# Attention in units of four steps instead of pairs, with the other products gathered in one slot of two

## Chip, core and metric

The kernel runs on one core of a Trainium2 chip. The metric is the device time of one execution in microseconds (us). Before the change it is 806.05 us, the median of 3 runs (804.99 to 806.32).

## The reference

The input x is 2 batches of 2048 tokens of 256 values, float32. All arithmetic is in float32.

```python
x = x + layernorm(attention(layernorm(x)))      # layernorm inside, 4 heads of 64, q and k RMS-normed
x = x + layernorm(ffn(layernorm(x)))
# attention: softmax(qn kn^T) v for each head and batch, then w_o and b_o
# ffn: scores = x gate_w^T; chosen = argmax over 8 experts; x + x expert_w[chosen]^T
```

The feed-forward part sends each token through one expert of eight, so tokens have to be sorted by expert before full tiles of them can be multiplied.

## The kernel before, in words

There are two paths, chosen by a test on the gains of q and k; the one that runs is `bounded_path`, and only this one is meant below. The scores are bounded there, so that the softmax needs no maximum: `exp(s - bound)` is summed as it comes.

**Attention.** One step is a batch, a block of 512 queries, a pair of heads and a tile of 128 keys: 2 x 4 x 2 x 16 = 256 steps. `scores` (L1034) issues a step's two matmuls on TensorE, one for each head, each over 64 rows (tile s, two buffers of two banks), and the exponential on ScalarE that makes the tile p (five buffers). `add` (L1075) adds p into acc on VectorE; acc's column sums become the softmax's denominators. `weigh` (L1087) issues the step's two matmuls with the values, each into 64 of the rows of po (one bank, summed over 16 steps). A float32 matmul appears in the trace as two records, so a step has four records of s and four of po. After 16 steps po is copied to oT (L1129), and `block_sums` (L1051) takes acc's sums with a ones matrix (tile sm, L1056), and in four parts the reciprocals and the products with oT on VectorE.

**Other work.** The remaining work is cut into Python generators that stand in a queue with a slot number at which they begin: `project` (norm, products for q, k and v and their transposes, for one tile of tokens: 32 in all), `expert_weights`, `tokens` (after two blocks of heads: the output projection py on TensorE, the norm, the choice of the expert on VectorE, in two parts one slot apart; in the last rows of a group one tile of tokens per slot, otherwise one in four), `order` (the routing of a group: the matmuls rank, a chain of small VectorE instructions, a slot later a second chain, and later the matmuls src), `places` (one tile of tokens of one expert: gather, transposes pt_g, product pe, norm) and `collect` (gather of the finished rows, residual, output). Group A is the first batch, group B the first three blocks of the second. `between` (L926) is one slot: it moves each running generator one step on. A step ends at a `yield`; a `yield then(...)` runs on in the same slot, a `yield later(...)` or a bare `yield` ends the slot for that generator. The `Next` that a yield gives names the engine of the next step, its cost and what it takes. Before the change only the planner of the end (`finish`, L944) uses it.

**The order.** The engines' order is the order in which the code issues (a manual schedule), and each engine works through its own queue in that order. The loop at L1111 runs over pairs of steps. In each round it issues the scores of the next pair, the adds of the present pair, one slot of other work, and the values of the present pair:

```python
ahead = [scores(i) for i in following]
for i, p in zip(mine, held):
    add(i, p)
between(now)
now += 1
for i, p in zip(mine, held):
    weigh(i, p)
held = ahead
```

Other matmuls share three banks (`ps_m`, L344). After the last pair, `finish` plans what is left by estimated costs.

Of the kernel before, what the change touches and what calls it, by code (L numbers as in the profile page):

```python
# [25 lines left out]
def kernel(  # L26
# [23 lines left out]
    NT = N // P  # L50
# [223 lines left out]
    def bounded_path():  # L274
# [76 lines left out]
        class Next(NamedTuple):  # L351
# [8 lines left out]
            give: str = ""  # L360
            later: bool = False
            order: int = -1

        then = Next

        def later(*args, **kw):
            return Next(*args, later=True, **kw)
# [58 lines left out]
        def project(bt, t):  # L426


            n = f"{bt.b}_{t}"
            src = x_tile(bt.b * NT + t)  # L430

            mv, _ = moments(src, f"a{n}")
            rs = roots[:, bt.b * NT + t : bt.b * NT + t + 1]
            rsqrt(rs, mv[:, 1:2], 1.0 + LN_EPS, LN_EPS * LN_EPS, ALU.add)
            yield
            xn = wk.tile([P, D], F32, tag="xn", name=f"xn_{n}")
            nc.vector.tensor_scalar(xn, src, mv[:, 0:1], rs, ALU.subtract, ALU.mult)
            yield
            pt = ps_m(f"pt_x{n}")
            for c in range(NCH):  # L440
                nc.tensor.transpose(  # L441
                    pt[:, c * P : (c + 1) * P], xn[:, c * P : (c + 1) * P], ident
                )
            xnT = wk.tile([P, NCH, P], F32, tag="xnT", name=f"xnT_{n}")
            nc.scalar.activation(  # L445
                xnT,
                pt[:, :D].rearrange("p (c n) -> p c n", n=P),
                AF.Identity,
                bias=raised,
            )  # L450
            yield
            pqk = ps_m(f"pqk{n}")
            for c in range(NCH):
                nc.tensor.matmul(  # L454
                    pqk,
                    xnT[:, c, :],
                    wqkT[:, c, :, :].rearrange("p a d -> p (a d)"),
                    start=(c == 0),
                    stop=(c == NCH - 1),
                )  # L460
            pv = ps_m(f"pv{n}")
            for c in range(NCH):
                nc.tensor.matmul(  # L463
                    pv[:, :DG],
                    xnT[:, c, :],
                    wvT[:, c, :],
                    start=(c == 0),
                    stop=(c == NCH - 1),
                )
            qk = wk.tile([P, 2 * D], F32, tag="qk", name=f"qk_{n}", bufs=4)  # L470
            nc.scalar.copy(qk, pqk)  # L471
            nc.scalar.copy(bt.V[:, t, :], pv[:, :DG])
            sq = wk.tile([P, 2 * D], F32, tag="sq", name=f"sq_{n}", bufs=1)
            nc.scalar.activation(sq, qk, AF.Square)
            yield
            ss = small.tile([P, 2 * H], F32, tag="ss", name=f"ss_{n}")
            nc.vector.tensor_reduce(
                ss, sq.rearrange("p (g d) -> p g d", d=DH), AX.X, ALU.add
            )
            rn = small.tile([P, 2 * H], F32, tag="rn", name=f"rn_{n}")  # L480

            rsqrt(rn, ss, 1.0 / DH, RMS_EPS * RMS_EPS, ALU.max)
            yield
            qk3 = qk.rearrange("p (g d) -> p g d", d=DH)
            nc.vector.tensor_tensor(
                qk3, qk3, rn.unsqueeze(2).to_broadcast([P, 2 * H, DH]), ALU.mult
            )
            yield
            pt = ps_m(f"pt_qk{n}")
            for c in range(2 * NCH):  # L490
                nc.tensor.transpose(  # L491
                    pt[:, c * P : (c + 1) * P], qk[:, c * P : (c + 1) * P], ident
                )
            cols = bass.ts(t, P)
            qb, j = divmod(t, QT4)
            if bt.QT[qb] is None:
                bt.QT[qb] = kv.tile([P, NCH, KB], F32, tag="QT", name=f"QT{n}", bufs=NKB + 1)
            pt3 = pt.rearrange("p (c n) -> p c n", n=P)
            qt = bt.QT[qb][:, :, bass.ts(j, P)]
            nc.scalar.activation(  # L500
                bt.KT[:, :, cols], pt3[:, NCH : 2 * NCH, :], AF.Copy, scale=g_k
            )
            if bt.b == 0:
                nc.vector.tensor_scalar(qt, pt3[:, :NCH, :], g_q8, None, ALU.mult)
            else:
                nc.scalar.activation(qt, pt3[:, :NCH, :], AF.Copy, scale=g_q8)
            bt.done.add(t)
            yield

        def expert_weights(e):  # L510
            w = load_raw(raw, expert_w[e], f"we_raw{e}")
            yield
            yield
            wt = raw.tile([P, NCH, D], F32, tag="wraw", name=f"weT{e}")
            turn_weight(w, four(ps_m(f"pt_we{e}")), wt)

            for c in range(NCH):
                own = wt[:, c, c * P : (c + 1) * P]
                nc.vector.tensor_tensor(own, own, ident, ALU.add)
            nc.sync.dma_start(out=weTd[e], in_=wt)  # L520
            yield
# [51 lines left out]
        def order(gr):  # L573
# [3 lines left out]
            ps = ps_m(f"rank{n}")  # L577
# [31 lines left out]
            end = tiles  # L609
            k = 1  # L610
            while k < E:
# [3 lines left out]
                end = more  # L615
# [54 lines left out]
            ps = ps_m(f"src{n}")  # L670
# [15 lines left out]
            for t in range(T):  # L686
                at += 0.5 if at >= len(steps) // PAIR + lead else 1
                g = opens(early(collect(gr, t)), Next("POOL", 1.3), 3, lambda: None if gr.left else gr.written)
                queue.append((at + 4, g))
            queue.sort(key=lambda q: q[0])  # L690
            yield

        def places(gr, j):
# [18 lines left out]
            nc.sync.dma_start(  # L712
                out=w, in_=weTd[bass.ds(e, 1)].rearrange("e p c d -> p (e c) d")
            )
            yield later("PE", 0.3, 3.0, take="mx")
            if attending:
                yield later("PE", 0.3, take="mx", give="mx")
            pt = ps_m(f"pt_g{n}")
            for c in range(NCH):
                nc.tensor.transpose(  # L720
# [202 lines left out]
                if step is None or step is running or step.later:  # L923
                    return step is not running

        def between(now):  # L926
            new = []
            while queue and queue[0][0] <= now:
                new.append(queue.pop(0)[1])
                if new[-1] in firsts:  # L930
                    advance(new[-1])
            old = running[:]
            running.extend(new)
            due = old + [g for g in new if g not in firsts]
            begun.update((g, now) for g in new)


            if 3 < now < NT + 4 or now == 2:
                due.sort(key=lambda g: max(2 - now + begun[g], -1) % 4)
            for g in due:  # L940
                if not advance(g):
                    running.remove(g)

        def finish():  # L944

# [84 lines left out]
        def ready(i):  # L1030
            b, qb, c, kc = steps[i]
            return batches[b].done.issuperset({kc, *range(qb * QT4, (qb + 1) * QT4)})
# [74 lines left out]
        while not all(ready(i) for i in range(PAIR)):  # L1107
            between(now)
            now += 1
        held = [scores(i) for i in range(PAIR)]  # L1110
        for g in range(len(steps) // PAIR):  # L1111
            mine = range(g * PAIR, (g + 1) * PAIR)
            following = [i + PAIR for i in mine if i + PAIR < len(steps)]
            while not all(ready(i) for i in following):
                between(now)
                now += 1
            lead = now - g
            ahead = [scores(i) for i in following]
            for i, p in zip(mine, held):
                add(i, p)  # L1120
            between(now)
            now += 1
            for i, p in zip(mine, held):
                weigh(i, p)
            held = ahead
            b, qb, c, kc = steps[mine[-1]]
            if kc == NT - 1:
                oT = wk.tile([P, KB], F32, tag="oT", name=f"oT{g}", bufs=4)
                nc.scalar.copy(oT, po)  # L1129
                w = opens(block_sums(g, acc, oT), Next("PE", 1.0, take="m"), 0)  # L1130
                queue.append((now, w))
                oTs.append(oT)
                if c == NCH - 1:
                    tt = b * NT + qb * QT4
                    gr = next((g for g in groups if g.first <= tt < g.first + g.T), None)
                    last = gr and tt + QT4 == gr.first + gr.T
                    gap = 1 if last else 4 if following else 1
                    for j in range(QT4):
                        w = tokens(batches[b], qb, j, oTs, gr)
                        end = (len(steps) // PAIR - 1, j)  # L1140
                        opens(w, Next("PE", 0.5, take="m"), 0, lambda end=end: normed.get(end))
                        queue.append((now + 1 + gap * j, w))
                    oTs = []
                queue.sort(key=lambda q: q[0])
# [380 lines left out]
```

## Time and profile before

| what | us |
|---|---|
| median of 3 runs | 806.05 |
| the profiled execution's own time | 805.99 |
| its span, first to last instruction | 804.2 |
| PE busy / DVE busy / ACT busy / POOL busy | 760.8 / 639.4 / 448.8 / 326.2 |
| one exponential p (ACT, 256 of them) | 1.110 |
| one add into acc (DVE, 224 of them) | 1.222 |
| one reciprocal of 128x128 (DVE, 64 of them) | 0.95 |
| TensorE clock granted, mean | 0.978 |

PE is TensorE's matmuls, PEld its weight loads, DVE is VectorE, ACT ScalarE, POOL GpSimd, SP the engine that issues most of the transfers. A row of a timeline gives the start and the length of a group of like instructions in us, the engine, the line, what is written from what, how often, and in brackets how long the engine sat idle before and what ended that. A matmul's length is that of one instruction from its start to its end; since matmuls are pipelined, the step from one start to the next is what it costs.

### The profile page before, as it was taken

What the parts mean: (1) busy time and instruction counts of PE and PEld (TensorE: products, weight loads), DVE (VectorE), ACT (ScalarE), POOL (GpSimd) and SP (SyncE); (2) the same over time, 40 slices, a digit from 0 to 9 for tenths busy, and PEclk for the clock granted to TensorE, in tenths of its full rate; (3) what the DMA queues carried; (4) which work ended last, traced back from release to release, by engine and by line L of the source; (5) the groups of instructions that cost most, each with busy time, mean ns of one, the idle gap of its engine ahead of it and who ended that gap; (6) DMA issues with size and microseconds to landing.
All of it is one profiled execution on the core that took longest, in us unless ns stands there. A gap on an engine that the chain in (4) does not pass through costs nothing.

```text
span 804.2 us, 10268 instructions
## 1 busy us (share of the span) xinstructions
PE 760.8 (95%) x3166; PEld 320.4 (40%) x3166; DVE 639.4 (80%) x1379; ACT 448.8 (56%) x699; POOL 326.2 (41%) x336
## 2 busy tenths in 40 slices
PE   7999999999999999999997999999999996997794
PEld 5545433343334333433332434444443332334551
DVE  2757688789797879688989976878698899975767
ACT  2656655555656555655554455666666543355851
POOL 3634331134253344244324135757545445127114
PEclk8999999999999999999999999999999999899997
DMA  4100211210010000000131413433212343317436
GB/s 128 54 1 26 66 54 52 79 33 20 13 54 15 13 20 20 21 20 20 48 110 60 119 33 105 125 112 112 73 48 77 112 118 98 109 53 255 88 105 193
DMA packets 48686, 57.58 MB, mean 72 GB/s; under 512 B 6408, under 2 KB 39952, under 8 KB 48624
## 3 DMA queue, kind: packets, MB, share of 16 engines
q1 hardware_dynamic: 42064, 44.65, 17.4%
q0 software_dynamic: 3568, 9.32, 4.7%
q10 hardware_dynamic: 2992, 2.88, 1.2%
q8 instruction: 27, 0.44, 0.2%
q14 instruction: 35, 0.29, 0.1%
HBM read 37.69 MB, written 19.14 MB: 71 GB/s over the span
## 4 chain that ended last, share of the span: by engine, by line
PE 75%; DVE 12%; ACT 3%; DMA 3%; issue 3%; POOL 2%; SPq 0%; DVEq 0%; POOLq 0%; ACTq 0%
PE s L1040 24%; PE po L1094 24%; PE pqk L454 7%; PE pv L463 4%; DVE acc L1085 3%; PE peA L730 3%; PE py L793 3%; PE pt_qk L491 2%; PE sm L1056 2%; PE peB L730 1%; PE pt_x L441 1%; DVE acc L1064 1%; PE pe L862 1%; DMA fgA<-fnA,posA 1%; ACT p L1048 1%
## 5 line engine op out<-in xcount | busy, mean ns | idle before, releaser
L1048 ACT ACTIVATE p<-s,nbound 128x1024 f32<-128x1024 f32 x256 | 271.0, 1110 | 182.7 <-PE s L1040 182.7
L1085 DVE TENSOR_TENSOR acc<-acc,p 128x1024 f32<-128x1024 f32 x224 | 273.6, 1222 | 11.5 <-ACT p L1048 1.2
L1040 PE MATMUL s<-QT,KT 64*128 64x512 f32 x1024 | 255.1, 616 | 2.3 <-ACT p L1048 2.3
L1094 PE MATMUL po<-p,V 128*64 128x512 f32 x1024 | 251.5, 612 | 0.2 <-ACT oT L1129 0.2
L1040 PEld LDWEIGHTS s<-QT,KT 64*128 64x128 f32 x1024 | 88.3, 187 | 165.2 <-issue 92.2
L1094 PEld LDWEIGHTS po<-p,V 128*64 128x64 f32 x1024 | 64.1, 138 | 129.2 <-issue 126.9
L374 POOL TENSOR_TENSOR rn<-rs_t,mhalf 128x8 f32<-128x8 f32 x32 | 58.8, 1839 | 74.1 <-DVE rs_t L373 74.1
L374 POOL TENSOR_TENSOR roots<-rs_t,mhalf 128x1 f32<-128x1 f32 x32 | 23.9, 748 | 96.4 <-DVE rs_t L373 96.3
L454 PE MATMUL pqk<-wqkT,xnT 128*128 128x512 f32 x128 | 62.0, 608 | 0.3 <-ACT xnT L445 0.3
L374 POOL TENSOR_TENSOR rs_z<-rs_t,mhalf 128x1 f32<-128x1 f32 x28 | 34.8, 1243 | 59.0 <-DVE rs_t L373 59.0
L374 POOL TENSOR_TENSOR rs_y<-rs_t,mhalf 128x1 f32<-128x1 f32 x28 | 32.2, 1149 | 55.7 <-DVE rs_t L373 49.1
L1064 DVE RECIPROCAL acc<-acc 128x128 f32<-128x128 f32 x45 | 42.5, 944 | 0.0
L837 ACT ACTIVATE x2n<-x,shift_y,rs_y 128x256 f32<-128x256 f32 x28 | 16.8, 599 | 44.0 <-POOL shift_y L391 39.2
L698 POOL DMA_INDIRECT rows<-x2nA,srcA x23 | 29.9, 1298 | 24.3 <-DMA ring<-weTd 18.3
L793 PE MATMUL py<-woT,oT 128*128 128x264 f32 x128 | 35.6, 402 | 0.5 <-ACT xTB L725 0.5
L768 POOL DMA_INDIRECT fgA<-fnA,posA x16 | 19.9, 1243 | 37.9 <-DVE rs_t L373 12.0
L463 PE MATMUL pv<-wvT,xnT 128*128 128x264 f32 x128 | 33.7, 386 | 0.0
L1064 DVE RECIPROCAL acc<-sm 128x128 f32<-128x128 f32 x19 | 18.0, 950 | 18.7 <-PE sm L1056 18.7
L374 POOL TENSOR_TENSOR rs_fA<-rs_t,mhalf 128x1 f32<-128x1 f32 x23 | 18.1, 785 | 36.0 <-DVE rs_t L373 35.0
L471 ACT COPY qk<-pqk 128x512 f32<-128x512 f32 x32 | 18.8, 587 | 22.8 <-PE pqk L454 22.8
L463 PEld LDWEIGHTS pv<-wvT,xnT 128*128 128x128 f32 x128 | 24.3, 190 | 17.6 <-issue 10.8
L698 POOL DMA_INDIRECT rows<-x2nB,srcB x19 | 20.9, 1098 | 22.4 <-DVE srcB L679 16.8
(262 smaller groups left out, 927.9 us busy)
## 6 DMA issues: line engine op xcount, KB each, us to landing
ring<-weTd SPq DMA_DIRECT2D x34, 256.0 KB, 3.0
x<-in_L_attn_x_dram SPq DMA_DIRECT2D x8, 512.0 KB, 4.0
xr<-in_L_attn_x_dram SPq DMA_DIRECT2D x28, 128.0 KB, 2.2
fnA<-fA SPq DMA_DIRECT2D x23, 128.0 KB, 2.4
we_raw<-in_L_ffn_expert_w_dram ACTq DMA_DIRECT2D x8, 256.0 KB, 2.6
weTd<-weT SPq DMA_DIRECT2D x8, 256.0 KB, 2.1
x2A<-x SPq DMA_DIRECT2D x16, 128.0 KB, 1.7
fgA<-x2A SPq DMA_DIRECT2D x16, 128.0 KB, 2.1
```

Source lines behind the costliest of these rows:

```text
L374: nc.gpsimd.tensor_tensor(dst, t[:, :n], mhalf[:, :n], ALU.pow)
L454: nc.tensor.matmul(pqk, xnT[:, c, :], wqkT[:, c, :, :].rearrange("p a d -> p (a d)"), start=(c == 0), stop=(c == NCH - 1),)
L463: nc.tensor.matmul(pv[:, :DG], xnT[:, c, :], wvT[:, c, :], start=(c == 0), stop=(c == NCH - 1),)
L698: nc.gpsimd.indirect_dma_start(out=xg, out_offset=None, in_=gr.x2n[:, :], in_offset=bass.IndirectOffsetOnAxis(ap=gr.src[:, j : j + 1], axi ...
L730: nc.tensor.matmul(pe, xT[:, c, :], w[:, c, :], start=(c == 0), stop=(c == NCH - 1))
L768: nc.gpsimd.indirect_dma_start(out=o, out_offset=None, in_=gr.fn[:, :], in_offset=bass.IndirectOffsetOnAxis(ap=gr.pos[:, t : t + 1], axis= ...
L793: nc.tensor.matmul(py, oT[:, bass.ts(j, P)], woT[:, c, :], start=(c == 0), stop=(c == NCH - 1),)
L1040: nc.tensor.matmul(s[:, r, :], bt.KT[rows, c, bass.ts(kc, P)], bt.QT[qb][rows, c, :], start=True, stop=True,)
L1048: nc.scalar.activation(p, s, AF.Exp, bias=nbound)
L1064: nc.vector.reciprocal(acc[:, 0, cols], share[:, cols])
L1085: nc.vector.tensor_tensor(acc, acc, p, ALU.add)
L1094: nc.tensor.matmul(po[r * DH : (r + 1) * DH, :], batches[b].V[:, kc, h * DH : (h + 1) * DH], p[:, r, :], start=(kc == 0), stop=(kc == NT - 1),
```

## The change

The loop now runs over units of four steps: the scores of two steps, then the adds that the unit before left over, one slot of other work ("few"), the scores of two more steps, the adds of the first two, the values of all four, and one more slot ("rest"). The adds of the last two steps are issued in the next unit after its first scores, or, at the end of a block of 16 steps, directly after the slot "rest". In a slot "few" the steps whose engine is PE go ahead up to three banks or until 2.0 us of estimated work are there; what doesn't fit is put off, and only that goes in the slot "rest". Steps of other engines go in both. As long as the first batch is projected (slots below 20) every slot takes all, and there are two more slots in a unit, among the values.

For this, some steps say that they begin on PE and what they take; `places` waits one slot without a bank in place of holding one, and `collect` begins four slots later.

```diff
+            banks: int = 1
...
             xn = wk.tile([P, D], F32, tag="xn", name=f"xn_{n}")
             nc.vector.tensor_scalar(xn, src, mv[:, 0:1], rs, ALU.subtract, ALU.mult)
-            yield
+            yield later("PE", 0.3)
...
-            yield
+            yield later("PE", 2.7, banks=2)
             pqk = ps_m(f"pqk{n}")
...
-            yield
+            yield later("PE", 0.5)
             pt = ps_m(f"pt_qk{n}")
...
             yield
-            yield
+            yield later("PE", 0.6)
             wt = raw.tile([P, NCH, D], F32, tag="wraw", name=f"weT{e}")
...
-                queue.append((at + 4, g))
+                queue.append((at + 8, g))
...
-            yield later("PE", 0.3, 3.0, take="mx")
             if attending:
-                yield later("PE", 0.3, take="mx", give="mx")
+                yield later("", 0.0, 3.0)
+                yield later("PE", 0.3, take="mx")
+            else:
+                yield later("PE", 0.3, 3.0, take="mx")
             pt = ps_m(f"pt_g{n}")
...
-        def between(now):
+        def between(now, kind="all"):
+            nonlocal put_off
...
+            banks, work, waiting = 0, 0.0, set()
             for g in due:
+                step = nexts.get(g) or opening.get(g)
+                if kind != "all" and step and step.engine == "PE":
+                    full = banks + step.banks > 3 and work < 2.0
+                    if full if kind == "few" else g not in put_off:
+                        waiting.add(g)
+                        continue
+                    banks, work = banks + step.banks, work + step.cost
                 if not advance(g):
                     running.remove(g)
+            put_off = waiting if kind == "few" else set()
...
-        held = [scores(i) for i in range(PAIR)]
-        for g in range(len(steps) // PAIR):
-            mine = range(g * PAIR, (g + 1) * PAIR)
-            following = [i + PAIR for i in mine if i + PAIR < len(steps)]
-            while not all(ready(i) for i in following):
-                between(now)
-                now += 1
-            lead = now - g
-            ahead = [scores(i) for i in following]
-            for i, p in zip(mine, held):
+        added = []
+
+        def slot(kind="all"):
+            nonlocal now
+            between(now, kind if now >= NT + 4 else "all")
+            now += 1
+
+        for g in range(len(steps) // (2 * PAIR)):
+            mine = range(g * 2 * PAIR, (g + 1) * 2 * PAIR)
+            while not all(ready(i) for i in mine):
+                slot()
+            lead = now - 2 * g
+            ps = [scores(i) for i in mine[:PAIR]]
+            for i, p in added:
                 add(i, p)
-            between(now)
-            now += 1
-            for i, p in zip(mine, held):
+            slot("few")
+            ps += [scores(i) for i in mine[PAIR:]]
+            for i, p in zip(mine[:PAIR], ps):
+                add(i, p)
+            projecting = now < NT + 4
+            if projecting:
+                slot()
+            for i, p in zip(mine[:PAIR], ps):
                 weigh(i, p)
-            held = ahead
+            if projecting:
+                slot()
+            for i, p in zip(mine[PAIR:], ps[PAIR:]):
+                weigh(i, p)
+            added = list(zip(mine[PAIR:], ps[PAIR:]))
+            slot("rest")
...
             if kc == NT - 1:
                 oT = wk.tile([P, KB], F32, tag="oT", name=f"oT{g}", bufs=4)
                 nc.scalar.copy(oT, po)
+                while added:
+                    add(*added.pop(0))
                 w = opens(block_sums(g, acc, oT), Next("PE", 1.0, take="m"), 0)
```

More of the change, by code (lines that the diff above doesn't have):

```diff
@@ L939, in between @@
                 due.sort(key=lambda g: max(2 - now + begun[g], -1) % 4)
+            banks, work, waiting = 0, 0.0, set()
             for g in due:
+                step = nexts.get(g) or opening.get(g)
[5 more added lines that the diff above has]
+                    banks, work = banks + step.banks, work + step.cost
                 if not advance(g):
                     running.remove(g)
+            put_off = waiting if kind == "few" else set()
+        put_off = set()
         def finish():
@@ L1109, in bounded_path @@
             now += 1
-        held = [scores(i) for i in range(PAIR)]
-        for g in range(len(steps) // PAIR):
-            mine = range(g * PAIR, (g + 1) * PAIR)
-            following = [i + PAIR for i in mine if i + PAIR < len(steps)]
-            while not all(ready(i) for i in following):
-                between(now)
-                now += 1
-            lead = now - g
-            ahead = [scores(i) for i in following]
-            for i, p in zip(mine, held):
-                add(i, p)
-            between(now)
-            now += 1
-            for i, p in zip(mine, held):
-                weigh(i, p)
-            held = ahead
+        added = []
[10 more added lines that the diff above has]
+            for i, p in added:
+                add(i, p)
+            slot("few")
[6 more added lines that the diff above has]
+            for i, p in zip(mine[:PAIR], ps):
+                weigh(i, p)
+            if projecting:
[4 more added lines that the diff above has]
+            slot("rest")
+            following = mine[-1] + 1 < len(steps)
             b, qb, c, kc = steps[mine[-1]]
@@ L1139, in bounded_path @@
                         w = tokens(batches[b], qb, j, oTs, gr)
-                        end = (len(steps) // PAIR - 1, j)
+                        end = (len(steps) // (2 * PAIR) - 1, j)
                         opens(w, Next("PE", 0.5, take="m"), 0, lambda end=end: normed.get(end))
```

## The prediction

> **What bounds the kernel now.** The page comes first: busy time by engine, and the span in 40 slices (a digit is the busy share in tenths).
>
> ```profile
> PE 760.8 (95%) x3166; PEld 320.4 (40%) x3166; DVE 639.4 (80%) x1379; ACT 448.8 (56%) x699; POOL 326.2 (41%) x336
> ...
> PE   7999999999999999999997999999999996997794
> ...
> DVE  2757688789797879688989976878698899975767
> ```
>
> PE is the bound from slice 2 to about 36 (the attention); the dips to 7 and 6 are the places where it waits. So a change in the attention pays by what PE does between useful matmuls, and costs by new waits in PE's queue. The timeline of PE and of its weight loads in an ordinary stretch shows the first (start, length, engine, line):
>
> ```profile
> 401.86 1.94 PE L1094 MATMUL po<-p,V 128*64 128x512 f32 x8
> 403.72 1.99 PE L1040 MATMUL s<-QT,KT 64*128 64x512 f32 x8
> 405.64 1.08 PE L1056 MATMUL sm<-acc,ones 128*64 128x512 f32 x4
> 406.55 1.89 PE L1094 MATMUL po<-p,V 128*64 128x512 f32 x8
> 408.37 1.99 PE L1040 MATMUL s<-QT,KT 64*128 64x512 f32 x8
> ```
>
> ```profile
> 403.72 0.30 PEld L1040 LDWEIGHTS s<-QT,KT 64*128 64x128 f32 x4 [0.81 <-ACT p L1048]
> 404.26 0.19 PEld L1040 LDWEIGHTS s<-QT,KT 64*128 64x128 f32 x2 [0.23 <-issue]
> 404.69 0.19 PEld L1040 LDWEIGHTS s<-QT,KT 64*128 64x128 f32 x2 [0.23 <-issue]
> 405.64 0.20 PEld L1056 LDWEIGHTS sm<-acc,ones 128*64 128x64 f32 x4 [0.76 <-issue]
> ```
>
> Records start in pairs, 7 ns apart. Inside a block a pair starts every 0.43 us (404.26, 404.69), so four pairs are 1.72. The block of s takes 1.92 from start to next start. PE has three shapes: s (64*128), po and sm (128*64), all else (128*128, F below). The po block that follows sm, its own shape, takes 1.82; the one that follows s takes 1.86. Over all single records, leaving a shape costs 0.094 us whatever comes next; entering s costs 0.098 more, entering po or sm 0.045, entering F 0.055 with transposes first and 0.104 with products first. So a switch into s costs 0.191, into po/sm 0.138, into F 0.148 or 0.197.
>
> The waits: PE's own waits are small and sit on DVE at the two routing points. Timeline of PE, then of DVE, there:
>
> ```profile
> 431.64 1.99 PE L1040 MATMUL s<-QT,KT 64*128 64x512 f32 x8
> 437.79 0.77 PE L579 MATMUL rankA<-picksA,before 128*128 128x128 f32 x2 [4.16 <-DVE picksA L271]
> ...
> 438.92 3.04 PE L1094 MATMUL po<-p,V 128*64 128x512 f32 x8
> ...
> 445.68 1.99 PE L1040 MATMUL s<-QT,KT 64*128 64x512 f32 x8
> 448.42 1.08 PE L1056 MATMUL sm<-acc,ones 128*64 128x512 f32 x4 [0.75 <-DVE acc L1085]
> ```
>
> ```profile
> 437.41 0.23 DVE L271 TENSOR_SCALAR picksA<-eidx,first 128x8 f32<-128x8 f32 x1
> ...
> 438.30 2.54 DVE L1085 TENSOR_TENSOR acc<-acc,p 128x1024 f32<-128x1024 f32 x2
> 440.76 0.28 DVE L589 COPY countA<-rankA 128x128 f32<-128x128 f32 x1
> ...
> 445.81 2.55 DVE L1085 TENSOR_TENSOR acc<-acc,p 128x1024 f32<-128x1024 f32 x2
> 448.28 0.32 DVE L631 TENSOR_TENSOR slA<-end_A,col 128x161 f32<-128x161 f32 x1
> ...
> 453.98 1.22 DVE L1083 TENSOR_TENSOR acc<-p,p 128x1024 f32<-128x1024 f32 x1
> ```
>
> Here DVE is the bound: the sums sm wait for the last two adds of the block (445.81), and the second half of the routing work (448.28 to 453.98, 5.70 us) stands behind those adds and costs PE nothing. That order is what the change turns round.
>
> **Gain: switches.** The order in which the built programs issue PE's instructions (no times in it) gives, from the first s to the last po: before 126 switches into s, 128 into po/sm, 95 into F (48 with transposes first); after 121, 82, 64 (32). At the prices above: before 24.1+17.7+7.1+9.3 = 58.1; after 23.1+11.3+4.7+6.3 = 45.5. Gain 12.6 us, 0.22 per unit of four steps. In about seven units at the two routing points DVE sets the pace and a faster PE only waits longer: 1.7 off, 10.9 stays. No matmul is added or removed.
>
> **Cost 1: sums behind the routing, the main one.** After: the adds of a unit's last two steps stand on DVE behind all the work of the "rest" slot, and the sums' matmul stands on PE in the next "few" slot, between two s blocks; PE's queue is in order, so s, po and all else wait with it. At group A the order is: picks, two adds, count work, two adds, second half of routing, two adds, sm. From the last pick the chain before is 448.42-437.79 = 10.6; after, 5.70 and one more pair of adds (445.81 to 448.28, 2.47) come ahead of sm: 18.8. PE gets there with rank, an s block, four steps of po and an s block: 0.7+1.92+3.57+1.92 = 8.1, so nothing hides it. +8.2. At group B the same rows are 4.84 (692.57 to 697.41) and 2.47: +7.3. The picks themselves: DVE has almost no gap from the previous sm to them in both orders; by the sum of its rows with the new order, its wait for py included, they come 0.4 (A) and 0.9 (B) earlier. Net +14.2.
>
> After a wait PE is slow for a while: 3.04 for the po block at 438.92 against 1.94, 1.1 us lost after 4.16 idle; at B, after 5.16 idle, po 3.68 and s 2.10, 1.85 lost. The Trainium skill ("TensorE: Matmul & The Clock Gate", "What's actually happening") speaks against the change here: an idle window of about 3.4 us halves the clock until a window that long is busy, so 1.7 per gap, 3.4 for two. No row shows a gap of 9 us; the two rows give 1.1 and 1.85. I take 1.4 each, +2.8, as the losses of the rank waits fall inside DVE's time now as before. Bounds 0 and 4.
>
> **Cost 2: sums elsewhere.** From the start T of a unit's second s block: py ends at T, DVE makes y to rs_t of a token (0.43+0.43+0.18+0.15) by T+1.35, two adds 2.47, the token's second half (2.39 by its ten rows), two adds: T+8.7. PE is at sm at T+1.92+3.57+1.92 = T+7.4 plus what other products stand ahead. The order shows six more block ends with a token in the last unit and little ahead of sm: waits of 1.3, 1.3, 0.7, 1.25, 1.25 and 1.7, 7.5 in all; 0.9 off because DVE's rows overlap by some 5%; before had 1.14 of it (the sm at 646). +5.5; bounds 2 and 9. At the other ends 2.6 us of products or an idle DVE cover it; without that cover 1.3 each.
>
> **Cost 3: two s blocks with nothing between.** Six units have an empty few slot. s has two buffers:
>
> ```profile
> 409.60 2.12 ACT L1048 ACTIVATE p<-s,nbound 128x1024 f32<-128x1024 f32 x2 [1.37 <-PE s L1040]
> ```
>
> The s block before this began at 408.37, so the exponentials end 2.29 and 3.35 after it; the next s could begin after 1.82 and its second half 0.86 later. It waits 0.5 and then 0.2: +4.2 for six; bounds 0 and 5. Elsewhere at least 0.4 us of F and two switches cover it. The second exponentials have the po of two steps (1.8) as cover; ACT's other work of the slot (1.5 to 4 us by the order) starts with the products, so most of it is done when the second s is. I take 0; if that cover is gone, 0.3 per unit.
>
> **Cost 4: the rest.** Two tiles' expert products and one tile's transposes move behind the attention: 8 records of 0.216 and 2 of 0.11, 1.9 us, on a tail that is partly ACT and DVE: +1.5; bounds 0 and 3. places' waits move to an empty step and collect's start moves four slots; both groups' gathers and their DMAs on SP and POOL still issue within the attention, where neither queue is the bound: 0. A token's load xr goes out on SP with py and is read 3.8 us later by the sum of cost 2; it lands in 2.2: 0, and without that cover 2.2 per token. The projecting units have as many products: 0.
>
> Sum on the profiled execution, 805.99 (its span 804.2, 1.8 around it, within 0.1 of the median): -10.9+14.2+2.8+5.5+4.2+1.5 = +17.3, 823.3.
>
> **Rivals.** (a) Faster: PE isn't held at the two routing sums, because DVE has caught up when PE arrives. Place: sm after rankA and rankB; price 17.0; it decides once DVE is ready within 9 us of the last pick instead of 18.8. With the lesser waits at their low bounds too (2, 0 and 0): -12.6+2 gives 795. For it: 12.6 is firm, priced from hundreds of switches. Against: the order puts 5.70 and two adds ahead of sm, with DVE full already. Chance 0.07. (b) Only the routing waits are real and the rest is covered: -10.9+14.2+2.8 = +6, 812. For: before, PE waited for sums only three times. Chance 0.15. (c) ACT's queue: x2n waits for POOL (39.2 us of ACT idle in the page), and in the new order it stands ahead of the second two exponentials, with po behind them. At 0.3 per unit in some 57 units, 17 more: 840. For: the cover is 1.8 where it was a block of po and the other products. Against: most units have none, as the shift is 2.3 us of POOL begun a whole s block earlier. Chance 0.11. (d) The sum above: 0.67.
>
> **Numbers.** Predicted 823. The range reaches down to (b) and, upwards, to the bounds of costs 1 to 4 that can come together: 809 to 832. About 0.2% (1.6 us) is what a measurement of this kernel can tell from no change. Faster 0.07, within it 0.03, slower 0.90.
>
> **What would show it.** PE busy falls by about 12; po blocks have 16 records in 3.57 us. The sm after rankA and rankB waits 8 to 11 us for DVE acc; six other sm wait about 1; s after s waits for ACT p six times. Wrong would be: sm waits under 3 us at the routing points, or po waiting for ACT p in most units.

## The result and the profile after

The changed kernel takes 844.75 us, the median of 4 runs (843.43 to 847.32), beside 806.12 of the kernel before (4 runs, 804.99 to 806.32): a ratio of 1.049, 95% interval 1.0467 to 1.0512. (The ratios here and below are of the means of the unprofiled executions, so they differ a little from the quotient of the medians.) The profiled execution took 845.63, its span is 843.9, 39.7 longer than before.

From the page of the changed kernel, busy time by engine, then PE and its granted clock in 40 slices of the span:

```profile
PE 768.1 (91%) x3166; PEld 327.2 (39%) x3166; DVE 642.0 (76%) x1378; ACT 452.8 (54%) x706; POOL 316.9 (38%) x332
...
PE   6999899999999999999976999999999885987695
...
PEclk9999999999999999999997999999999897799598
```

PE has the same 3166 records, so nothing was added. Its row is 9 through most of the attention as before; lower than before are slices 21 and 22 (7 and 6 for 9 and 7: group A's routing) and 32 to 34 (8, 8, 5 for 9, 9, 6: a block's end at 661 and group B's routing). Behind the attention the clock is new: 5 in slice 38. Two numbers split the 39.7: the last values of the last block end at 727.4 before and at 753.4 after, which puts **+25.9 into the attention**, and from there to the end it is 76.8 before and 90.5 after, **+13.7 behind it**.

An ordinary stretch of the changed kernel, PE's timeline:

```profile
404.59 1.99 PE L1057 MATMUL s<-QT,KT 64*128 64x512 f32 x8
407.87 1.08 PE L1073 MATMUL sm<-acc,ones 128*64 128x512 f32 x4 [1.29 <-DVE acc L1102]
408.88 1.99 PE L1057 MATMUL s<-QT,KT 64*128 64x512 f32 x8
410.79 3.65 PE L1111 MATMUL po<-p,V 128*64 128x512 f32 x16
414.38 1.99 PE L1057 MATMUL s<-QT,KT 64*128 64x512 f32 x8
416.29 2.05 PE L796 MATMUL py<-woT,oT 128*128 128x264 f32 x8
418.27 1.99 PE L1057 MATMUL s<-QT,KT 64*128 64x512 f32 x8
```

The values of four steps are one block, 3.59 from its start to the next start (410.79 to 414.38), and a unit has one block of other products. The saved switches are there. So is their price: this unit begins a block of 16 steps, its first product is sm, and it waits 1.29 for the adds of the block before. Where such waits fall is told by PE's waits (total us, times, longest):

```profile
PE sm L1073 <- DVE acc L1102: 26.0, 8, 8.3
PE peB L733 <- ACT xTB L728: 5.8, 6, 1.2
PE pt_gB L723 <- ACT spare L743: 5.3, 7, 2.0
PE rankB L580 <- DVE picksB L271: 4.1, 1, 4.1
PE po L1111 <- ACT p L1065: 3.7, 3, 1.6
PE rankA L580 <- DVE picksA L271: 3.3, 1, 3.3
```

Before, sm had waited 1.9 in all. The second and third row are not of the attention: they are the expert tiles in the plan of the end. At group A's routing the PE timeline shows the longest kind of wait,

```profile
440.00 0.76 PE L580 MATMUL rankA<-picksA,before 128*128 128x128 f32 x2 [3.29 <-DVE picksA L271]
...
441.12 3.79 PE L1057 MATMUL s<-QT,KT 64*128 64x512 f32 x8
444.84 4.17 PE L1111 MATMUL po<-p,V 128*64 128x512 f32 x16
448.94 1.99 PE L1057 MATMUL s<-QT,KT 64*128 64x512 f32 x8
459.16 1.98 PE L1073 MATMUL sm<-acc,ones 128*64 128x512 f32 x4 [8.24 <-DVE acc L1102]
461.07 2.92 PE L1057 MATMUL s<-QT,KT 64*128 64x512 f32 x8
```

and DVE's timeline shows what it waits for:

```profile
449.70 1.23 DVE L1102 TENSOR_TENSOR acc<-acc,p 128x1024 f32<-128x1024 f32 x1 [0.46 <-ACT oT L1161]
450.85 0.32 DVE L632 TENSOR_TENSOR slA<-end_A,col 128x161 f32<-128x161 f32 x1
...
454.15 2.49 DVE L663 TENSOR_TENSOR inrowA<-rowA,col 128x512 f32<-128x512 f32 x4
456.56 2.55 DVE L1102 TENSOR_TENSOR acc<-acc,p 128x1024 f32<-128x1024 f32 x2
461.18 0.96 DVE L1081 RECIPROCAL acc<-sm 128x128 f32<-128x128 f32 x1 [2.08 <-PE sm L1073]
```

The second half of the routing (450.85 to 456.56) stands ahead of the block's last two adds, and sm behind those. Then DVE idles 2.08 itself, until sm is done. PE is slow after such a wait: sm takes 1.98 for four records that take 1.08 elsewhere, the block of s behind it 2.92 for eight that take 1.99 (granted clock 0.72 from 459 to 466).

Behind the attention. Before, the expert tiles were taken several at a time; PE's timeline of the kernel before:

```profile
745.66 2.76 PE L730 MATMUL peB<-ring,xTB 128*128 128x256 f32 x12
748.26 0.38 PE L720 MATMUL pt_gB<-ident,rows 128*128 128x128 f32 x2
748.99 0.44 PE L720 MATMUL pt_gB<-ident,rows 128*128 128x128 f32 x2 [0.35 <-ACT fB L405]
750.99 0.44 PE L720 MATMUL pt_gB<-ident,rows 128*128 128x128 f32 x2 [1.57 <-ACT xTB L725]
751.44 5.41 PE L730 MATMUL peB<-KT,xTB 128*128 128x256 f32 x16
```

After, one at a time:

```profile
785.95 0.69 PE L723 MATMUL pt_gB<-ident,rows 128*128 128x128 f32 x2 [0.46 <-ACT spare L743]
786.89 2.08 PE L733 MATMUL peB<-KT,xTB 128*128 128x256 f32 x4 [0.26 <-ACT xTB L728]
789.58 0.69 PE L723 MATMUL pt_gB<-ident,rows 128*128 128x128 f32 x2 [0.61 <-ACT spare L406]
791.03 2.08 PE L733 MATMUL peB<-KT,xTB 128*128 128x256 f32 x4 [0.77 <-ACT xTB L728]
793.57 0.69 PE L723 MATMUL pt_gB<-ident,rows 128*128 128x128 f32 x2 [0.46 <-ACT spare L743]
795.49 2.07 PE L733 MATMUL peB<-KT,xTB 128*128 128x256 f32 x4 [1.23 <-ACT xTB L728]
```

A tile is two records of pt_gB, ScalarE's copy of them, four records of peB, and ScalarE's copy of those. Before, seven tiles' products (28 records) start within 745.66 to 756.69, 1.6 each, with three tiles' transposes among them. After, each tile's transposes wait for the copy of the tile before and its products for its own, and a tile takes 3.6 to 4.5 (starts of pt_gB at 785.95, 789.58, 793.57, 798.03). PE also runs at half pace here: 2.08 for the four records that take 1.13 at 780.40. The windows view says the same of 30 us (busy us and records of PE, PEld, DVE, ACT, POOL, then the granted clock):

```profile
783.40:813.40 30.00, 25.08 (x64) 13.88 (x65) 17.15 (x76) 15.69 (x52) 0.00 (x0) 0.66 0.10 35
```

Over the whole end the same view has PE busy for 66.1 us at a mean clock of 0.86, before for 56.3 at 0.93. PE's waits there, summed from the single records, are 14.4, before 9.9. So of the 13.7 the waits are some 4.5 and the records that moved there 1.95; the greater part, an estimate from these figures, is PE's slow pace. It comes with this order: the clock of the end is 0.86 again in e7 below, which has the same order, and 0.92 in e6 and e8, which have nearly that of before.

### The profile page after: what moved, and what is told of

The parts are those of the page before. It is cut to its first block, busy times and chain, and to the rows that moved or that the text cites. A ratio compares the mean times of both kernels' runs of the same rounds, so it can differ in the third digit from the quotient of the medians.

```text
span 843.9 us, 10321 instructions
## 1 busy us (share of the span) xinstructions
PE 768.1 (91%) x3166; PEld 327.2 (39%) x3166; DVE 642.0 (76%) x1378; ACT 452.8 (54%) x706; POOL 316.9 (38%) x332
## 4 chain that ended last, share of the span: by engine, by line
PE 69%; DVE 20%; ACT 4%; issue 3%; DMA 2%; POOL 1%; SPq 0%; DVEq 0%; POOLq 0%; ACTq 0%
PE s L1057 22%; PE po L1111 20%; PE pqk L455 7%; DVE acc L1102 7%; PE pv L464 3%; PE py L796 3%; PE sm L1073 2%; PE pe L865 2%; PE peA L733 2%; PE peB L733 2%; PE pt_qk L492 2%; ACT p L1065 1%; DVE x L822 1%; DVE acc L1081 1%; DVE st_z L379 1%
## 5 line engine op out<-in xcount | busy, mean ns | idle before, releaser
L1057 PE MATMUL s<-QT,KT 64*128 64x512 f32 x1024 | 265.4, 638 | 1.9 <-ACT p L1065 1.9
L1111 PE MATMUL po<-p,V 128*64 128x512 f32 x1024 | 237.1, 602 | 3.7 <-ACT p L1065 3.7
L1057 PEld LDWEIGHTS s<-QT,KT 64*128 64x128 f32 x1024 | 90.6, 192 | 148.4 <-issue 94.3
L1111 PEld LDWEIGHTS po<-p,V 128*64 128x64 f32 x1024 | 67.0, 137 | 165.6 <-issue 148.3
L375 POOL TENSOR_TENSOR rs_z<-rs_t,mhalf 128x1 f32<-128x1 f32 x28 | 32.1, 1148 | 118.1 <-DVE rs_t L374 117.4
L699 POOL DMA_INDIRECT rows<-x2nA,srcA x23 | 33.3, 1448 | 34.5 <-DVE srcA L680 28.6
L1073 PE MATMUL sm<-acc,ones 128*64 128x512 f32 x64 | 20.0, 706 | 26.1 <-DVE acc L1102 26.0
L375 POOL TENSOR_TENSOR roots<-rs_t,mhalf 128x1 f32<-128x1 f32 x32 | 22.1, 691 | 36.7 <-DVE rs_t L374 36.6
L811 DVE TENSOR_TENSOR y<-py,bias_o 128x264 f32<-128x264 f32 x28 | 12.0, 429 | 30.6 <-PE py L796 30.6
L472 ACT COPY qk<-pqk 128x512 f32<-128x512 f32 x32 | 18.8, 586 | 26.1 <-PE pqk L455 26.1
L455 PEld LDWEIGHTS pqk<-wqkT,xnT 128*128 128x128 f32 x128 | 22.1, 193 | 23.4 <-issue 21.9
```

The source lines that it names most:

```text
L375: nc.gpsimd.tensor_tensor(dst, t[:, :n], mhalf[:, :n], ALU.pow)
L455: nc.tensor.matmul(pqk, xnT[:, c, :], wqkT[:, c, :, :].rearrange("p a d -> p (a d)"), start=(c == 0), stop=(c == NCH - 1),)
L699: nc.gpsimd.indirect_dma_start(out=xg, out_offset=None, in_=gr.x2n[:, :], in_offset=bass.IndirectOffsetOnAxis(ap=gr.src[:, j : j + 1], axi ...
L1057: nc.tensor.matmul(s[:, r, :], bt.KT[rows, c, bass.ts(kc, P)], bt.QT[qb][rows, c, :], start=True, stop=True,)
L1073: nc.tensor.matmul(sm[r * DH : (r + 1) * DH, :], ones, acc[:, r, :], start=True, stop=True)
L1111: nc.tensor.matmul(po[r * DH : (r + 1) * DH, :], batches[b].V[:, kc, h * DH : (h + 1) * DH], p[:, r, :], start=(kc == 0), stop=(kc == NT - 1),
```

## Experiments

The kernels ran in three groups: e1 to e4 on one chip, e5 to e8 and then e9 to e11 on another. In the first and third the kernel before stood at 817.7 and 818.0, in the second at 807.5, so it is not the chip alone. "End" below is the time from the end of the last values to the end of the span. The profiles of the first and third group have 8 to 10 us more there for the same order (e3 87.0 where the kernel before had 76.8, e11 98.8 where the changed kernel had 90.5), with waits of ScalarE and VectorE for nothing that the profile shows. So times and ends are compared within a group only. The last values differ less: in three profiles of the changed kernel, one in the result and one in each of the later groups, they end at 753.4, 751.0 and 750.1, so 3 us between groups mean nothing.

**Is it the sums' place? e1: the adds first.** At a block's end the last two adds are issued ahead of the slot "rest".

```diff
             added = list(zip(mine[PAIR:], ps[PAIR:]))
+            while added and steps[mine[-1]][3] == NT - 1:
+                add(*added.pop(0))
             slot("rest")
```

> The changed kernel, but at the end of each block of 16 steps the adds of the last two steps are issued ahead of the slot 'rest', not behind it. Theory (DVE's order): the sums' matmul no longer waits behind the slot's work. The sm waits of 1.3 us at the ordinary block ends go, and the two of 8.3 us at the routing points shrink by the 5.7 and 4.8 us of the routing's second half, to some 3 us each, with less slow clock after them: 18 to 22 us off 844.75, so 823 to 827; the tail stays near 91 us from the last po. Rival (the sums wait because DVE is full in any order): the waits only move, under 6 us off.

Measured: 839.62, ratio 1.0249 (1.0202 to 1.0296). The last values start at 740.3; in e2 below, which has the changed kernel's order up to the last block, they start at 752.7 in the same group: 12.4 earlier, for the 18 to 22 expected. The end is 98.6, not 91, as this group's ends are long. From its waits of PE, and its timeline at group A:

```profile
PE po L1111 <- ACT p L1065: 9.6, 10, 2.3
PE sm L1073 <- DVE acc L1102: 8.1, 2, 4.4
```

```profile
444.30 1.99 PE L1057 MATMUL s<-QT,KT 64*128 64x512 f32 x8
450.70 1.98 PE L1073 MATMUL sm<-acc,ones 128*64 128x512 f32 x4 [4.42 <-DVE acc L1102]
452.61 3.79 PE L1057 MATMUL s<-QT,KT 64*128 64x512 f32 x8
```

The six lesser sm waits are gone, those at the routing fall from 8.2 and 8.3 to 4.4 and 3.6, and seven more waits of po for ScalarE take 5.8 of it back. So the place of the last two adds is the cause of the sm waits, but not of all the loss: at the routing the count work and four adds stand ahead of sm in either order.

**Is the end's length part of the change? e2: no gathering in the last block.** The slots of the last four units take all, as before the change.

```diff
-            between(now, kind if now >= NT + 4 else "all")
+            between(now, kind if NT + 4 <= now and unit < 60 else "all")
 ...
         for g in range(len(steps) // (2 * PAIR)):
+            unit = g
```

> The changed kernel, but in the last four units each slot takes all steps again. So the attention hands the planner of the end about the state that the kernel before handed it, and the planned order of TensorE's matmuls in the tail is nearly that of before. Theory (the tail is long by the order planned for it, one expert tile at a time with two banks held by py): the tail goes from 91 us to 78 to 81, for some 1 us more in the attention: 832 to 836 in all. Rival (the tail is long because it has two tiles more to do and a slow clock): 1 to 3 us off, 842 to 844.

Measured: 843.78, ratio 1.0309 (1.0277 to 1.0342); the end is 89.0, above the 78 to 81 expected, but 9.6 shorter than the 98.6 of e1, with the last values no later than in the changed kernel. The gathering costs this time, through what it leaves for the plan of the end: less work done, and another order for it. Which of the two counts, e9 tells.

**Without the adds: e3 and e4.** In both kernels `add` returns from a block's third step on, so DVE is never late. This leaves out 14 of 16 steps' share of the denominators.

```diff
             else:
-                nc.vector.tensor_tensor(acc, acc, p, ALU.add)
+                return
```

> The kernel before without its adds from the third step of a block on (the softmax's denominators hold two steps of sixteen). DVE loses 224 adds of 1.22 us and isn't the bound anywhere. Both theories: the waits at the two routing points go, 12 to 18 us off 806, 788 to 794. It is the base for the next run.

> The changed kernel without the same adds (denominators of two steps of sixteen). What is left of the change is TensorE's order: 82 fewer switches of its array's shape, against it the waits of s for an exponential in the six units without other products, of po for an exponential, and the tail. Theory (DVE's order makes the attention's loss): from the first s to the last po it is 6 to 10 us shorter than the kernel before without adds; with the tail's 13 the whole is 3 to 7 us above that kernel. Rival (the values wait for exponentials whatever DVE does): the attention is no shorter, the whole 13 or more above.

Measured: e3 (the kernel before) 794.84, ratio 0.9706 (0.9666 to 0.9747); e4 (the changed one) 800.45, ratio 0.9778 (0.9748 to 0.9807). e3 is 22.8 below the kernel before of its group, more than the 12 to 18 expected. With the adds the change costs 38.6, without them 5.6; in the attention it costs 25.9 with them and nothing without. So the attention's loss hangs on the adds. But the attention, freed of every sm wait, gains only 2.2 (last values start at 704.6 and 706.8), and 1.95 of that are the records that moved behind it; my expectation of 6 to 10 is missed, and the 5.6 lies within the 3 to 7 only because the end grew by 6.8 and not by 13. By single records the switches save 12.7, and losses that have nothing to do with DVE's adds take 12.6 back: 6.8 where s follows s, 2.5 of po for exponentials, 1.5 of short losses around py, and 1.8 more, mostly in the projecting units. Two of e4's waits of PE:

```profile
PE po L1111 <- ACT p L1065: 1.7, 2, 1.1
PE s L1057 <- ACT p L1065: 1.7, 4, 0.4
```

The brackets show less than the loss: an s block with a wait of 0.4 costs 0.85 from start to start, as its second half waits again, and two of the six cost 1.7.

**One part alone: e5 and e6.** The loop over pairs of the kernel before, with the changed steps and products gathered in every other slot ("few", "rest"); e6 takes all in the last eight pairs.

```diff
-            between(now)
+            between(now, "all" if now < NT + 4 or g >= LAST else "few" if g % 2 == 0 else "rest")
```

LAST is never reached in e5 and 120 in e6. (In a slot "few" a step is put off only where it would go over three banks while under 2.0 us of work are there; once 2.0 us are there, nothing more is put off.)

> One part of the change alone: the loop over pairs of the kernel before (next scores, adds, one slot, values), with the other products gathered in one slot of two as in the change. DVE's order at the block ends is then that of before: the sums wait for their own adds, with the routing's second half behind them. The order has 52.3 us of switches at the measured prices (58.1 before, 45.5 after), and at the end it hands the planner the state that the changed kernel hands it: the planned order of PE's matmuls in the tail is the changed kernel's but for one tile. Theory (units of four bring the attention's loss by DVE's order, the planned order brings the tail's): the attention is 3 to 6 us shorter than before, the tail as long as the changed kernel's, 1.006 to 1.012 of before in all. Rival (gathering itself makes the sums late): the sm waits at the two routing points are 5 us or more and the whole is over 1.025.

> As the run before it, but in the last eight pairs each slot takes everything again, so that the planned order of PE's matmuls in the tail is nearly that of the kernel before. Theory: 9 to 13 us less than the run before it, nearly all of it after the last po, and so 0.991 to 0.998 of the kernel before. Rival (the tail's length isn't the planned order): within 3 us of the run before it.

Measured: e5 816.3, ratio 1.0112 (1.0073 to 1.015), e6 804.3, ratio 0.9956 (0.9936 to 0.9976). Both have the attention shorter than the kernel before (last values end at 718.5 and 722.5, where it was 727.4), as the gathering saves some 5 us of switches (52.7 and 53.2 for 58.5, at the prediction's prices), 1.95 of records move behind it in e5, and no sm is moved: sm waits for the adds once in e5, 0.6, and never in e6. They differ behind it: the end is 91.4 in e5 and 79.9 in e6. PE's timeline of e6 there, with products in blocks of three and four tiles again, as before the change:

```profile
743.57 2.76 PE L733 MATMUL peB<-ring,xTB 128*128 128x256 f32 x12
...
749.35 5.41 PE L733 MATMUL peB<-KT,xTB 128*128 128x256 f32 x16
```

The eight pairs cost 4.0 in the attention and save 11.4 at the end. **e6 is 0.4% faster than the kernel before**: in pairs of steps the gathering pays a little; in units of four it doesn't, even with both mends (e8).

**The changed kernel with both mends: e7 and e8.** e7 is the changed kernel again, e8 has the edits of e1 and e2.

> The changed kernel unaltered, on the same chip as the runs sent with it, since chips were seen to differ by a dozen us. Every theory: about 1.049 times the kernel before, as on the first chip; its tail after the last po is the measure for the other tails of this call.

> The changed kernel with the two earlier mends together: adds ahead of the slot 'rest' at block ends, and all steps in every slot of the last four units. If the two causes are apart, what they take off adds: 18 and 10 us, so 1.013 to 1.018 of the kernel before. What is left above it is the waits at the routing points, of s and po for exponentials, and some 3 us at the beginning. If both mends work on the same thing it stays above 1.022.

Measured: e7 847.96, ratio 1.0529 (1.0491 to 1.0567), with an end of 91.0 and sm waits of 25.8 in all as in the first profile; e8 824.56, ratio 1.022 (1.0199 to 1.024). The mends add up to 23.4: 8.2 at the last values and 12.2 in the end, by the two profiles; the rest lies in e7's spread (843.68 to 854.32). e8 is still 2.2% above the kernel before, above my expectation and at the edge of the rival's 1.022, since the adds' place gave 8.2 where 18 was expected: 15.3 of its 17 are in the attention, where sm still waits 4.4 and 3.6 at the routing and po 9.6.

**What makes the end long? e9, e10, e11.** The two tiles of products more could do it, or the order in which the plan then takes the tiles. e9 runs one more slot after the last values, e10 moves one single tile on by a step, and the plan starts from there: no instruction of the attention and none of the work left over changes, only the order behind it. e11 is the changed kernel.

```diff
+        between(now - 1, "all")      # e9; in e10: advance(running[0])
         attending = False
         more_room()
         finish()
```

> The changed kernel, with one more slot of other work after the last values of the last block, before the plan of the end begins. The attention is the changed kernel's, instruction for instruction, and so is the work handed over: only the state from which the plan starts is another, and the plan then takes the expert tiles in runs of up to three (by the order in which the program issues them: three products, three transposes, three products) where the changed kernel takes eight of them one at a time. Theory (the end is long because the plan alternates one product and one transpose, each waiting for ScalarE): from the last values to the end 80 to 85 us where the changed kernel has 91.1 to 91.6, ratio 1.036 to 1.044 on a chip where the changed kernel stands at 1.049 to 1.053. Rival (the end is long because two tiles more are left over and start late): nothing changes, 90 to 92, ratio 1.047 to 1.055.

> The changed kernel, with one expert tile alone moved on by one step before the plan of the end begins. Attention and work handed over are the changed kernel's. By the order issued, the plan begins with runs of three products and falls back to one at a time for three tiles and to runs of two after that. Theory of the plan's order: between the two, 83 to 89 us from the last values to the end, ratio 1.040 to 1.050. Rival (work left over): 90 to 92, ratio 1.047 to 1.055.

> The changed kernel once more, for the comparison on the same chip: from the last values to the end 91 to 92 us, ratio 1.047 to 1.055. Both theories expect the same.

Measured: e9 842.43, ratio 1.0306 (1.0246 to 1.0366); e10 852.44, 1.0436 (1.0384 to 1.0488); e11 849.44, 1.041 (1.0342 to 1.0477). The ends are 84.8, 95.3 and 98.8. In e9's PE timeline tiles stand in twos and threes,

```profile
785.28 1.95 PE L733 MATMUL peB<-KT,xTB 128*128 128x256 f32 x8
787.65 1.17 PE L723 MATMUL pt_gB<-ident,rows 128*128 128x128 f32 x6 [0.41 <-ACT spare L743]
788.65 1.99 PE L733 MATMUL peB<-KT,xTB 128*128 128x256 f32 x8
```

and its end is 14.1 shorter than e11's with the same work: with nothing else left over, the order alone shortens it. How much is not settled by this pair, as e11's own end missed what was expected (91 to 92): PE ran at half pace early in it too (2.07 for four records at 755.85, a mean clock of 0.79 over the end, 0.92 in e9). Beside the 90.5 and 91.0 that the changed kernel's order took in the other groups, e9's 84.8 is about 6 shorter. So the order is worth 6 to 14. Even across the groups the profiles agree. Where the products of the 19 tiles left come in 12 groups, one tile at a time for long, the ends are 90.5, 91.0, 91.4, 93.8, 98.6 and 98.8 (the changed kernel, e7, e5, e4, e1, e11); where 17 to 19 tiles come in 7 or 8 groups, they are 76.8, 78.7, 79.9, 84.8, 87.0 and 89.0 (the kernel before, e8, e6, e9, e3, e2).

In time only 7.0 of the 14.1 shows, as e9's profile has the attention 6.8 longer than e11's with the same instructions up to there: 2.0 by the end of the first block, 3.1 at group A's routing and 1.8 at group B's. At A sm waited 9.4 there, and the clock was low again later: the 16 records of s at 473.49 take 6.4 to the next block, where the changed kernel's first profile has 4.5. e10, with 9 groups, missed the end that I expected (83 to 89): it is 3.6 shorter than e11's and the time no better. Its profile has waits that belong to no order:

```profile
ACT sd_f L396 <- issue: 8.9, 1, 8.9
...
PE py L796 <- issue: 5.5, 2, 4.4
```

e2 and e3 have such a wait of sd_f too, of 9.8 each, and ends some 10 longer than the same orders elsewhere (78.7 in e8, 76.8 in the kernel before). So e10 tells neither for nor against.

## Why the prediction was wrong

The direction was right and the mechanism of the main cost too; the size was wrong by 21.7 (844.75 for 823.0), and 832 had been the upper end. That the rival of ScalarE's queue, at 840, stands nearest is chance: its waits did not come. By the prediction's own steps, on the profiled executions (39.7 in all, 17.3 predicted):

- **Switches.** Priced with the prediction's costs at the counts of the trace, 58.5 before and 45.8 after, the first switch and the last included: 12.7 saved, where 12.6 was priced and 10.9 kept. This checks the counts, not the prices. The 1.7 taken off for the routing was not lost: the rank waits, with the waits for an exponential just ahead of them and the slow blocks behind, take about 15.4 in both.
- **Cost 1, the sums behind the routing.** The mechanism as told. From rank to sm it is 19.2 (440.00 to 459.16), for 18.8 from the last pick; the waits are 8.2 and 8.3, predicted as 8 to 11. With the slow blocks behind them the two cost 21.7, less 2.4 that the same sums cost before: +19.3 for 17.0. Nearly all of the 2.3 is the clock: 0.90 (sm) and 0.93 (s) at A, 0.90 (sm), 1.80 (s) and 0.34 (po) at B, 4.9 in all, with a granted clock of 0.72 from 459 to 466 and 0.60 from 716 to 724. I took 2.8; the estimate from the rule of the Trainium skill that the prediction weighed ("TensorE: Matmul & The Clock Gate", "What's actually happening") was 3.4. Both were low here, the rule's less so.
- **Cost 2, six other sums.** Six waits there were: 1.28, 1.31, 0.70, 1.29, 1.73 and 3.07. Predicted 7.5 before the deductions, measured 9.4; and the last, at 661.74, left PE slow, which lost 2.9 more. By single records the six cost 12.6, less 1.6 that such sums cost before: +11.0 for 5.5, mechanism right, size half.
- **Cost 3, s after s.** +5.7 for 4.2: the mechanism as told, a little larger. Rival (c), ScalarE's queue, is out: po waits for it three times, 3.7 in all, not in 57 units.
- **Cost 4, the rest, is the step that failed.** It put 1.5 on "a tail that is partly ACT and DVE", from 1.9 us of records moved there, and so took the plan of the end, and PE's pace in it, as fixed. The end grew by 13.7, the largest miss of any term. The runs put in its place: the gathering hands the plan another state (two tiles at their products and two at transposes, where before five tiles stood at five different steps), from it the plan takes tiles one at a time, and PE waits for ScalarE and runs slowly between them. e6, e8 and e2 restore about the state of before, order and work, and get back 11.4, 12.2 and 9.6; e9 keeps the work, changes the order alone, and gets back 6 to 14. The order in which the program issues PE's instructions had shown the alternation; I counted its instructions and did not read how they followed one another. In the attention cost 4 also missed 2.2 in the projecting units, 1.5 of short losses around py, and 1.3 of po for exponentials, and gained 1.95 by the records that left.

The sum of these: -12.7 + 19.3 + 11.0 + 5.7 + (2.2 + 1.5 + 1.3 - 1.95 - 0.3 for an earlier start) + 13.7 = 39.75, for 39.7 measured. The terms within the attention are worked out from single records with modelled ends and may be off by a few tenths each; the two stages' own differences, 25.9 and 13.7, are read off.

Of what "would show it", PE's busy time rose from 760.8 to 768.1 in place of falling by 12: busy time counts a slow block at its full length, so it is no measure of switches once the clock differs. Rival (a) needed DVE to be ready within 9 us of the last pick; it needed 19. What inside the plan makes it alternate (the counts of buffers that it keeps, or only the phase in which the tiles arrive) was not tried apart and stays open, and so does what set off the slow pace at 783.60.

## What to carry over

Gathering work of one kind to save switches is worth no more than the switches cost (5 us of 806 in pairs, and e6 is 3 us faster), and only as long as no result is asked for in a queue before the work that makes it: the last adds put behind a slot's work, with the sums' matmul in the very next slot, lost 30.3 (19.3 and 11.0) where all switches saved 12.7. When an order is changed, compare the state that it leaves for the next stage, not only the work: here a planned end took 13.7 longer over nearly the same instructions, and by e9 their order alone is worth at least 6. And read an order as a sequence (A B A B against A A A B B B), since here each alternation waited for the engine in between (0.3 to 1.2 us a time in the rows above).

## What the runs showed of the hardware

A wait of TensorE can cost more than itself, and the added loss is not in proportion to the wait: after 1.73 idle (624.91) the next blocks ran at full pace, after 3.07 (661.74) they lost 2.9, after 8.2 and 8.3 they lost 1.8 and 3.0, and after 9.4 in e9 and 9.6 in e2 about 5, in pieces over the next 20 us. Waits of one length can differ: after 3.29 (rankA at 440.00) the blocks of s and po lost 2.3, after 3.26 at the same place in e1 (437.42) the block of s took 1.99, full pace. A stretch without any wait above 1.23 can be slow as well: from 783.60 to 801.68 in the changed kernel, where 2 us of products alternate with 2 us of short work and waits, the granted clock was 0.51. Much the same alternation ran at 1.00 in the 30 us before (753.4 to 783.4), so the pattern alone does not set the pace; what does was not tried. PE's timeline around the wait of 3.07:

```profile
661.74 1.98 PE L1073 MATMUL sm<-acc,ones 128*64 128x512 f32 x4 [3.07 <-DVE acc L1102]
663.65 3.79 PE L1057 MATMUL s<-QT,KT 64*128 64x512 f32 x8
667.36 3.84 PE L1111 MATMUL po<-p,V 128*64 128x512 f32 x16
```

On the same chip the kernel before stood at 807.5 in one group of runs and 818.0 in the next (ends of the changed kernel 91.0 and 98.8, though its median moved only from 847.96 to 849.44), with waits for nothing that the profile shows on ScalarE, VectorE and TensorE behind the attention. What they wait for was not settled.
